# Two transformer blocks on one core: identity products ahead of the first weights, another order of the first loads, another list of order numbers

## The chip, the cores and the metric

The kernel runs on one core of a Trainium2 chip. Its engines work side by side, each through its own list of instructions in order: TensorE (PE in the profile, with its weight loads as PEld), VectorE (DVE), ScalarE (ACT), GpSimd (POOL) and SyncE (SP), which here only issues DMAs. The metric is the device time of one execution in microseconds (us). The kernel before takes 1480.22 us, the median of 3 runs (1479.65 to 1481.72).

## The reference

The input x is 32 sequences of 128 tokens with 256 features, in float32. Two transformer blocks follow one another. Both have 16 heads of 16, and both are conditioned by one vector for each sequence.

```
# block 1 (L0)
mod = silu(cond) @ ada_w + ada_b                 # shift, scale, gate, twice
x = x + gate_sa * (attention(ln(x) * (1 + scale_sa) + shift_sa) @ sa_proj_w + b)
x = x + cross_attention(ln(x), ctx, mask) @ ca_proj_w + b
x = x + gate_ff * (gelu((ln(x) * (1 + scale_ff) + shift_ff) @ fc1_w + b) @ fc2_w + b)
# block 2 (L1)
x = x + attention(adaln1(x, cond), rope on q and k) @ sa_out_w
x = x + cross_attention(adaln2(x, cond), ctx, rope) @ ca_out_w
x = x + (gelu(adaln3(x, cond) @ ffn_w1 + b) @ ffn_w2 + b)
```

## The kernel before

The batch is cut into 16 groups of two sequences, 256 tokens each. Eight streams are under way at a time. A stream carries one group through one block and then takes the next group, so that there are 32 passes (16 groups, two blocks). The second block's weights replace those of the first in the same tiles after the last use in the first block.

One pass has these steps. `normed_T` (line 527) makes the layer norm: statistics on VectorE, the power of -1/2 on GpSimd, the normalised `y` on VectorE (line 547), four transposes on TensorE (line 559), and the modulated copy `xt` (lines 577 and 579). `rows_T` (line 598) multiplies weights by `xt`, for q and k and for the first layer of the feed-forward; `values` (line 610) makes v. `attention` does the scores twice for each of the two sequences: once for the row maxima (lines 723 and 735), which a small transpose (line 748) turns and line 752 subtracts inside q, and once more for the exponentials (line 761). Line 769 multiplies the exponentials by the values. `over_sums` (line 780) divides by the sums: line 787 gathers the sums by DMA, line 792 takes the reciprocals, line 795 writes them to DRAM, line 800 reads them back with a broadcast in two DMAs, and line 803 multiplies. `project` (line 813) multiplies by the output weights (line 836). `fed_forward` is the last part.

**The order is made by a planner inside the kernel's own Python.** Each piece of work is a task, a generator that yields when it can start, on which engine, which slots it needs and its rank. `Clock` (line 41) keeps a planned time for each engine. It has a price for each instruction and each transfer, and `TURN` is added when TensorE goes from one kind of product to another (full; rows for the scores; columns for the exponentials by the values). `Tasks.run` (line 143) always takes the task that could start earliest on its engine. Among those that start about as early it takes the lowest rank. Instructions are issued in that order, so each engine's list is fixed when the kernel is built.

`ORDER` (line 35) disturbs this. The planned time is cut into stretches of `EVERY` = 40 us. Each stretch has a number in the list. At zero, the ranks are used as they are. Otherwise the number seeds a hash, which moves some tasks' ranks by -2 to +2, and its remainder by 4 picks the `patience`, the width of "about as early":

```python
at = int(min(t for e, t in clock.free.items() if e in ("pe", "dve", "act")) / EVERY)
seed = ORDER[at] if at < len(ORDER) else 0
patience = (0.02, 0.02, 0.3, 0.8)[seed % 4]
```

**The start.** SyncE issues the first loads at fixed places, ahead of all tasks: `rows` (line 284), the conditioning vector `embT_raw` (287), the column vectors `cols` (290), the first part of `ada_w` (313), the first group's x (317) and `qkv_w` (260, called from line 324). GpSimd makes the identity (line 328) and then fills the value tiles and the tiles for the maxima (lines 346 and 349); VectorE's first instruction is line 334, which needs `cols` and `rows`; ScalarE's is the silu of the conditioning vector (335), followed by copies of `rows` (353). `the_first` (line 461) multiplies `ada_w` by the silu in 16 products (line 448) for the first scale and shift. Then comes the first group's path through lines 547, 559, 579 and 598.

Of the kernel before, what the change touches and what calls it, by code (L numbers as in the profile page):

```python
# [10 lines left out]
F32 = mybir.dt.float32  # L11
U8 = mybir.dt.uint8
AF = mybir.ActivationFunctionType
ALU = mybir.AluOpType
# [3 lines left out]
P = 128  # L18
B, S, D, H, HD, DF = 32, 128, 256, 16, 16, 1024
KC = D // P  # L20
FC = DF // P
GB = 2
# [8 lines left out]
NEVER = 1e9  # L31
# [1 line left out]

EVERY = 40.0
ORDER = (
    200, 7, 0, 0, 0, 0, 297, 0, 0, 0, 0, 0, 0, 0, 0, 0, 129, 264, 0, 0, 0, 312, 0, 0, 0, 388, 0, 0, 109, 188, 182,
    0, 0, 0, 292, 58
)


class Clock:
# [1 line left out]


    HOP, DRAIN, TABLE, PACE = 0.06, 0.22, 1.28, 1.03
    TURN = {"full": 0.15, "rows": 0.1, "columns": 0.1}

    def __init__(self):
        self.free = dict.fromkeys(("pe", "dve", "act", "pool", "sp", "none"), 0.0)
# [7 lines left out]
    def use(self, engine, took, way="full"):  # L57

        if engine in ("exp", "gelu"):
            if engine != self.table:  # L60
                took += self.TABLE
                self.table = engine
            engine = "act"
        if engine == "pe":
            took = took * self.PACE + (self.TURN[way] if way != self.way else 0.0)
            self.way = way
        self.free[engine] = max(self.now, self.free[engine]) + took
        return self.free[engine] + (self.DRAIN if engine == "pe" else self.HOP)
# [154 lines left out]
def two_blocks(ctx: ExitStack, tc: tile.TileContext, a: dict, out: bass.AP):  # L223
    nc = tc.nc
# [4 lines left out]
    const = pool("const", 1)  # L229
# [3 lines left out]
    clock = Clock()  # L233
# [3 lines left out]
    mms = [psum.tile([P, 2 * GT], F32, name=f"products{i}") for i in range(3)]  # L237
# [24 lines left out]
    def weight(rows, cols, uses, *names):  # L262

        t = const.tile([P, rows // P, cols], F32, name=f"w_{names[0]}")

        def second():
            n = cols // len(names)
            for i, name in enumerate(names):
                load(t[:, :, i * n:(i + 1) * n], f"L1_xcond_{name}")
                end = clock.dma(6.0)  # L270
            return end

        return Weight(t, uses, second)
# [6 lines left out]
    w_fc1 = weight(D, DF, FC, "ffn_w1")  # L280
    w_fc2 = weight(DF, D, 1, "ffn_w2")

    rows = const.tile([P, C + 2], F32, name="rows")
    nc.sync.dma_start(out=rows, in_=a["rows"])

    embT = {name: const.tile([P, KC, B], F32, name=f"embT_{name}") for name in ("raw", "silu")}
    nc.sync.dma_start(out=embT["raw"], in_=a["cond_1024"])

    cols = const.tile([P, a["vectors"].shape[1]], F32, name="cols")
    nc.sync.dma_start(out=cols, in_=a["vectors"])  # L290
    for _ in range(3):
        clock.load(32)
    vectors, at = {}, 0
    for name in _VECTORS:
# [8 lines left out]
    c_fc1 = vectors["L0_xcond_fc1_b"]  # L303
    c_f1 = vectors["L1_xcond_ffn_b1"]


    ada_lo, late = w_fc1.t, w_fc2.t.rearrange("p (k n) d -> p k (n d)", k=KC)
    ada_hi = late[:, :, 0:2 * D]
    lnw = [late[:, :, 2 * D:], ada_lo[:, :, 0:2 * D], ada_hi]
    spare = [t.rearrange("p f n -> p (f n)") for t in ht]  # L310
    clock.slots["ht"] = [NEVER]
    src = a["L0_xcond_ada_w"].rearrange("(c p) n -> p c n", p=P)
    nc.sync.dma_start(out=ada_lo[:, :, 0:2 * D], in_=src[:, :, 0:2 * D])
    t_ada = clock.load(512)

    def load_x(t, src, g):
        nc.sync.dma_start(out=t, in_=src[g * GB:(g + 1) * GB].rearrange("b s d -> s b d"))

    def load_ctx(i, g):
        nc.sync.dma_start(out=cxs[i], in_=a["ctx_1024"].rearrange("(c p) n -> p c n", p=P)[:, :, g * GT:(g + 1) * GT])  # L320

    load_x(xs[0], a["x"], 0)
    t_x0 = clock.load(256)
    load(w_qkv.t, "L0_xcond_qkv_w")
    w_qkv.there[0] = clock.load(768)

    ident = const.tile([P, P], F32, name="ident")
    make_identity(nc, ident)
    neg_half = const.tile([P, GB], F32, name="neg_half")
    nc.gpsimd.memset(neg_half, -0.5)  # L330
    rope = const.tile([P, 2, 2, S], F32, name="rope")
# [127 lines left out]
    mods, gates, gates_at, biases = {}, {}, {}, {"fc2": r_fc2, "f2": r_f2}  # L459

    def the_first():
        t = max(t_ada, 6.5)
        scale = yield from modulation(t, 0, "sa_scale", ada_lo, "silu", c_ada, D, D, True)
        shift = yield from modulation(t, 0, "sa_shift", ada_lo, "silu", c_ada, 0, 0, False)
        mods["L0", "sa"] = scale, shift
# [198 lines left out]
    def plain(to, wm, w, src, t, bias):  # L664
        yield after(wm, w, t), "pe", "mm st", 3
        at = clock.take("st")
        st = sts[at]
        slot, ps, t = rows_T(w, 0, src, KC)
        there = Event()

        def move():
            yield t, "act", "", 1
            for c in range(KC):
                nc.scalar.activation(st[:, c, :], ps[:, c, :], AF.Identity, bias=bias[:, c:c + 1])
            end = clock.use("act", 0.84)
            clock.give("mm", slot, end)
            yield end, "sp", "", 1
            for e in range(2):
                nc.sync.dma_start(out=to[0:P:2, e:C:2, :], in_=st[64 * e:64 * e + 64, 0:KC, :])
                end = clock.dma(2.4)  # L680
            clock.give("st", at, there.add(end))

        tasks.spawn(move(), wm)
        return there

    def turned(to, wm, w, col, src, t):

        yield after(wm, w, t), "pe", "mm st", 3
        at = clock.take("st")
        st = sts[at].rearrange("p (a e) s -> p a e s", a=2)  # L690
        slot, ps, t = rows_T(w, col, src, KC)
        there = Event()

        def move():
            yield t, "dve", "", 1
            for b in range(GB):
                one = slice(b * S, (b + 1) * S)
                nc.vector.tensor_tensor(st[:, :, :, one], ps[:, :, one].unsqueeze(2).to_broadcast([P, 2, 2, S]), rope,  # L698
                                        ALU.mult)
            end = clock.use("dve", 1.25)  # L700
            clock.give("mm", slot, end)
            yield end, "pool", "", 1
            nc.gpsimd.tensor_tensor(st[:, 0], st[:, 0], st[:, 1], ALU.add)  # L703
            yield clock.use("pool", 1.27), "sp", "", 4
            for e in range(2):
                nc.sync.dma_start(out=to[2 * e:P:4, :, :], in_=st[:, 0, e, :])
                end = clock.dma(2.4)
            clock.give("st", at, there.add(end))

        tasks.spawn(move(), wm)  # L710
        return there

    def attention(wm, hd, masked, t, t_v, name, done):
# [66 lines left out]
        def over_sums():  # L780


            n, w = 4 * R, 4 * H * GT // P
            yield copied, "sp", "", 1
            o = ous[ou[0]]
            few = p_s.tile([P, w], F32, tag="few", name=f"few_{name}", bufs=3)
            nc.sync.dma_start(out=few, in_=o[1:P:8, :, :])
            at = clock.dma(2.2)
            nc.sync.dma_start(out=wm.xt, in_=o[0:P:2, :, :])
            clock.dma(2.0)  # L790
            yield at, "dve", "", 1
            nc.vector.reciprocal(few, few)
            yield clock.use("dve", 1.15), "sp", "", 1
            inv = dram2.tile([n, C * GT], F32, tag="inv", name=f"inv_{name}")
            nc.sync.dma_start(out=inv.rearrange("r (t w) -> (r t) w", w=w), in_=few)
            yield clock.dma(1.7), "sp", "", 1
            by = o[:, 0:KC, :]
            for c in range(2):
                half = inv[:, c * KC * GT:(c + 1) * KC * GT]
                nc.sync.dma_start(out=by[c:P:2, :, :], in_=half.unsqueeze(1).to_broadcast([n, 4, KC * GT]))  # L800
                at = clock.dma(2.2)
            yield at, "dve", "", 1.5
            nc.vector.tensor_tensor(wm.xt, wm.xt, by, ALU.mult)  # L803
            clock.give("ou", ou[0], done.add(clock.use("dve", 0.7)))
# [8 lines left out]
    def project(wm, x, lhs, n, w, ready, bias, gate, name):  # L813


        if bias is not None:
            bias = biases[bias]
        if gate is not None:
            y, gate = gate, ys[gate]
        if bias is not None:  # L820
            for b in range(GB):
                if gate is None:
                    nc.gpsimd.tensor_tensor(x[:, b, :], x[:, b, :], bias, ALU.add)
                else:
                    gb = p_s.tile([P, D], F32, tag="gb", name=f"gb_{name}_{b}", bufs=2)
                    nc.gpsimd.tensor_tensor(gb, gate[:, b, :], bias, ALU.mult)
                    nc.gpsimd.tensor_tensor(x[:, b, :], x[:, b, :], gb, ALU.add)
                    clock.use("pool", 0.7)
                clock.use("pool", 0.7)
# [64 lines left out]
    class Context:  # L894
# [5 lines left out]
        def fetch(self, wm):  # L900
            yield after(wm, w_kv, 0.0), "sp", "cx", 2
            self.slot = clock.take("cx")
            self.t = cxs[self.slot]
            load_ctx(self.slot, self.g)
            self.there.add(clock.dma(3.3))

    def attended(wm, at, x, masked, t, t_v, w, bias, gate, eps, mod, g, name, then, cx=None):

# [66 lines left out]
    def stream(wm, mine, loaded):  # L975

        while loaded:
# [12 lines left out]

            def next_x(i):
                load_x(xs[i], a["x"] if then < NG else middle, then % NG)
                return xs[i], clock.dma(3.3)

            if then is not None and clock.slot("x") < NEVER:
                other = clock.take("x")
# [111 lines left out]
```

## Time and profile before

| what | value |
|---|---|
| median of 3 runs | 1480.22 us |
| the profiled execution | 1490.8 us, its span 1488.7 us |
| granted TensorE clock, mean | 0.992 |
| weight loads of line 723, both kinds | 8192, 253.8 us |
| products of lines 598 and 836 with the feed-forward weights | 2048, 471.9 us |
| row maxima (line 735), VectorE | 256, 300.0 us |
| exponentials (line 761), ScalarE | 256, 248.2 us |

The profile is one execution; its span goes from the first to the last instruction. The 40 slices of the span show how evenly TensorE is used; a digit is the busy share in tenths.

```profile
PE   7998999999999999999999999999999999999998
DMA  6333223232223133133223241221223111212201
```

A row of the profile names the line of the kernel, the engine, the operation, and what is written and read (out<-in). Ends of products are modelled, since they are pipelined: consecutive products overlap in the rows.

### The profile page before, as it was taken

How to read it: one execution, taken by the hardware profiler on the slowest of the kernel's cores; microseconds unless marked ns; L12 is line 12 of the kernel's file. 1: busy time of each engine (PE TensorE's matmuls, PEld its weight loads, DVE VectorE, ACT ScalarE, POOL GpSimd, SP SyncE). 2: the span in 40 equal slices, each digit the busy share in tenths (PEclk: the TensorE clock that was granted, in tenths of full speed). 3: DMA queues.
4: the chain of work that ended last, by engine and by line, in shares of the span. 5: the costliest groups of instructions: out<-in, count | busy, mean ns of one | idle time of the engine just before them, and what ended most of it. 6: DMA issues, size and time to landing. Idle time of an engine off the chain costs nothing.

```text
span 1488.7 us, 39505 instructions
## 1 busy us (share of the span) xinstructions
PE 1441.7 (97%) x16992; PEld 1187.0 (80%) x16992; DVE 876.8 (59%) x1514; ACT 711.0 (48%) x1150; POOL 359.9 (24%) x498
## 2 busy tenths in 40 slices
PE   7998999999999999999999999999999999999998
PEld 6877778787888887887777887888788787887887
DVE  7664555545555545557468565566487557655531
ACT  6544545455555563544444534544444443544452
POOL 3031322421232322333123132122032121201110
PEclk9999999999999999999999999999999999999999
DMA  6333223232223133133223241221223111212201
GB/s 224 119 94 98 65 60 101 65 83 80 72 71 102 57 92 102 62 94 102 80 72 105 76 135 60 67 85 56 65 85 116 58 58 61 73 41 65 72 26 39
DMA packets 107358, 120.49 MB, mean 81 GB/s; under 512 B 11632, under 2 KB 82992, under 8 KB 107184
## 3 DMA queue, kind: packets, MB, share of 16 engines
q1 hardware_dynamic: 107184, 117.98, 25.7%
q8 instruction: 133, 2.18, 0.6%
q14 instruction: 41, 0.34, 0.1%
HBM read 54.92 MB, written 12.68 MB: 45 GB/s over the span
## 4 chain that ended last, share of the span: by engine, by line
PE 80%; DMA 7%; DVE 6%; SPq 2%; issue 2%; ACT 2%; POOL 1%; DVEq 0%; ACTq 0%; POOLq 0%
PE products L598 26%; PE products L836 22%; PE scores L723 15%; PE small L769 7%; PE products L610 6%; PE products L559 3%; DVE top L735 2%; DMA ou<-inv_a 1%; PE small L748 1%; ACT exp L761 1%; DVE xt L803 1%; DMA ou<-inv_d 1%; DMA ou<-inv_b 1%; PE products L448 1%; DVE y L547 1%
## 5 line engine op out<-in xcount | busy, mean ns | idle before, releaser
L761 ACT ACTIVATE exp<-scores 128x1024 f32<-128x1024 f32 x256 | 248.2, 1022 | 171.1 <-PE scores L723 161.3
L735 DVE TENSOR_REDUCE top<-scores 128x8 f32<-128x1024 f32 x256 | 300.0, 1214 | 45.1 <-PE scores L723 44.7
L598 PE MATMUL products<-xt,w_ffn_w 128*128 128x256 f32 x1024 | 238.5, 384 | 0.4 <-ACT ht L865 0.4
L836 PE MATMUL products<-w_ffn_w,ht 128*128 128x256 f32 x1024 | 233.4, 382 | 0.0
L836 PEld LDWEIGHTS products<-w_ffn_w,ht 128*128 128x128 f32 x1024 | 192.5, 191 | 28.5 <-issue 1.4
L598 PEld LDWEIGHTS products<-xt,w_ffn_w 128*128 128x128 f32 x1024 | 189.5, 190 | 31.9 <-issue 3.4
L723 PEld LDWEIGHTS scores<-qa,keys 32*128 32x128 f32 x4096 | 127.8, 188 | 52.4 <-issue 26.2
L865 ACT ACTIVATE ht<-products,cols 128x256 f32<-128x256 f32 x256 | 115.9, 473 | 105.6 <-PE products L598 104.6
L775 ACT COPY ou<-small 128x512 f32<-128x512 f32 x128 | 75.5, 590 | 189.3 <-PE small L769 187.6
L723 PE MATMUL scores<-qa,keys 32*128 32x128 f32 x4096 | 152.3, 285 | 10.1 <-DVE top L735 4.0
L723 PEld LDWEIGHTS scores<-keys,queries 32*128 32x128 f32 x4096 | 126.0, 186 | 37.7 <-issue 22.2
L723 PE MATMUL scores<-keys,queries 32*128 32x128 f32 x4096 | 150.5, 283 | 3.7 <-ACT exp L761 1.5
L769 PE MATMUL small<-exp,values 128*32 128x128 f32 x4096 | 138.4, 276 | 1.3 <-DVE qa L752 1.2
L703 POOL TENSOR_TENSOR st<-st 128x512 f32<-128x512 f32 x64 | 83.4, 1307 | 232.0 <-DVE st L698 211.2
L841 DVE TENSOR_TENSOR x<-products,x 128x512 f32<-128x512 f32 x64 | 44.1, 689 | 142.5 <-PE products L836 141.8
L598 PE MATMUL products<-xt,w_qkv_w 128*128 128x256 f32 x512 | 125.7, 392 | 0.8 <-DVE xt L579 0.8
L752 DVE TENSOR_TENSOR qa<-queries,small 128x512 f32<-128x512 f32 x128 | 86.9, 679 | 63.9 <-PE small L748 61.2
L769 PEld LDWEIGHTS small<-exp,values 128*32 128x32 f32 x4096 | 104.0, 109 | 24.0 <-issue 11.4
L598 PEld LDWEIGHTS products<-xt,w_qkv_w 128*128 128x128 f32 x512 | 96.7, 196 | 16.4 <-issue 2.0
L803 DVE TENSOR_TENSOR xt<-xt,ou 128x512 f32<-128x512 f32 x64 | 48.8, 762 | 93.9 <-DMA ou<-inv_a 32.5
L698 DVE TENSOR_TENSOR st<-products,rope 128x512 f32<-128x512 f32 x128 | 81.5, 684 | 13.7 <-PE products L598 9.7
L845 DVE TENSOR_TENSOR y<-products,y 128x512 f32<-128x512 f32 x32 | 22.1, 689 | 108.4 <-PE products L836 92.8
(109 smaller groups left out, 1761.6 us busy)
## 6 DMA issues: line engine op xcount, KB each, us to landing
xt<-ou SPq DMA_DIRECT2D x64, 256.0 KB
keys<-st SPq DMA_DIRECT2D x96, 128.0 KB
queries<-st SPq DMA_DIRECT2D x96, 128.0 KB
cxt<-in_ctx SPq DMA_DIRECT2D x32, 256.0 KB
x<-in_x SPq DMA_DIRECT2D x16, 256.0 KB
keys<-st SPq DMA_DIRECT2D x16, 256.0 KB
y<-gate_dram_sa SPq DMA_DIRECT2D x16, 256.0 KB
ou<-inv_a SPq DMA_DIRECT2D x32, 128.0 KB
```

The costliest lines, as they stand in the source:

```text
L598: nc.tensor.matmul(ps[:, c, :], lhsT=w.t[:, k, at:at + P], rhs=src[:, k, :], start=(k == 0), stop=(k == KC - 1))
L610: nc.tensor.matmul(ps[:, b, :], lhsT=src[:, k, b * S:(b + 1) * S], rhs=w.t[:, k, col:col + D], start=(k == 0), stop=(k == KC - 1))
L698: nc.vector.tensor_tensor(st[:, :, :, one], ps[:, :, one].unsqueeze(2).to_broadcast([P, 2, 2, S]), rope, ALU.mult)
L703: nc.gpsimd.tensor_tensor(st[:, 0], st[:, 0], st[:, 1], ALU.add)
L723: nc.tensor.matmul(sc[:, r, c * S:(c + 1) * S], lhsT=lhs(slice(32 * r, 32 * r + 32), c), rhs=rhs(slice(32 * r, 32 * r + 32), c), start=Tru ...
L735: nc.vector.tensor_reduce(top[:, r:r + 2, TOP:TOP + 2 * C:2], scs[slot][:, r:r + 2, :].rearrange("p r (c s) -> p r c s", s=S), AX.X, ALU.max)
L752: nc.vector.tensor_tensor(qa, q[:, :, cut], ps.unsqueeze(1).to_broadcast([P, C, S]), ALU.subtract)
L761: nc.scalar.activation(exps[pt][r // 2], scs[slot][:, r:r + 2, :], AF.Exp, scale=SCALE)
L769: nc.tensor.matmul(ats[at][32 * r:32 * r + 32, c * S:(c + 1) * S], lhsT=v[:, b, i:i + HD, :].rearrange("p d t -> p (d t)"), rhs=exps[pt][r ...
L775: nc.scalar.copy(ous[ou[0]][:, :, cut], ats[at].rearrange("p (c s) -> p c s", s=S))
L836: nc.tensor.matmul(ps[:, b, :], lhsT=lhs(k, b), rhs=w.t[:, k, :], start=(k == 0), stop=(k == n - 1))
L865: nc.scalar.activation(ht[f // (FC // 2)][:, f % (FC // 2), :], ps[:, 0, :], AF.Gelu, bias=b1[:, f:f + 1])
```

## The change

The change has four parts.

- Twelve products of the identity by itself are put on TensorE right after the identity is made. They write a products buffer that nothing reads before it is written again.
- The first loads go out in another order: `embT_raw`, `ada_w`, `rows`, the first x, `cols`, `qkv_w`.
- Prices of the planner are set anew: `TURN`, now by the kind that is left rather than entered; several transfers; and the earliest start of `the_first`, 5.5 for 6.5.
- `ORDER` is a new list, of 37 numbers, 26 of them not zero, where the old one has 36 with 12 not zero.

In `project` a task may also wait, in the planner only, for a bias row that has not been planned yet.

```diff
-    200, 7, 0, 0, 0, 0, 297, 0, 0, 0, 0, 0, 0, 0, 0, 0, 129, 264, 0, 0, 0, 312, 0, 0, 0, 388, 0, 0, 109, 188, 182,
-    0, 0, 0, 292, 58
+    6622, 0, 91896, 0, 27754, 24892, 69964, 0, 30721, 66120, 0, 41605, 0, 69433, 0, 43084, 27437, 27178, 72830,
+    16201, 38328, 98324, 37276, 0, 13032, 79752, 41486, 59529, 18013, 48897, 61204, 13263, 51033, 0, 0, 0, 0
...
-    TURN = {"full": 0.15, "rows": 0.1, "columns": 0.1}
+    TURN = {"full": 0.1, "rows": 0.15, "columns": 0.15}
...
-            took = took * self.PACE + (self.TURN[way] if way != self.way else 0.0)
+            took = took * self.PACE + (self.TURN[self.way] if way != self.way else 0.0)
...
-                end = clock.dma(6.0)
+                end = clock.dma(3.0)
...
+    nc.sync.dma_start(out=embT["raw"], in_=a["cond_1024"])
+    clock.load(32)
...
+    nc.sync.dma_start(out=ada_lo[:, :, 0:2 * D], in_=src[:, :, 0:2 * D])
+    t_ada = clock.load(512)
     rows = const.tile([P, C + 2], F32, name="rows")
     nc.sync.dma_start(out=rows, in_=a["rows"])
...
+    load_x(xs[0], a["x"], 0)
+    t_x0 = clock.load(256)
     nc.sync.dma_start(out=cols, in_=a["vectors"])
-    for _ in range(3):
+    for _ in range(2):
         clock.load(32)
...
     make_identity(nc, ident)
+
+    for _ in range(12):
+        nc.tensor.matmul(mms[0][:, 0:P], lhsT=ident, rhs=ident, start=True, stop=True)
...
-        t = max(t_ada, 6.5)
+        t = max(t_ada, 5.5)
...
             nc.sync.dma_start(out=few, in_=o[1:P:8, :, :])
-            at = clock.dma(2.2)
+            at = clock.dma(2.1)
             nc.sync.dma_start(out=wm.xt, in_=o[0:P:2, :, :])
-            clock.dma(2.0)
+            clock.dma(2.4)
...
-            yield clock.dma(1.7), "sp", "", 1
+            yield clock.dma(1.6), "sp", "", 1
...
-                at = clock.dma(2.2)
+                at = clock.dma(2.5)
...
-            bias = biases[bias]
+            if bias not in biases:
+                yield (lambda: 0.0 if bias in biases else NEVER), "none", "", 0
+            row = biases[bias]
```

Left out are the old places of the moved lines, the renaming of `bias` to `row` in its uses, and four more prices of transfers: 2.4 to 2.3 twice, for the moves of keys and queries (lines 680 and 707); 3.3 to 3.0 for the context; and 3.3 to 2.9 for the next x.

More of the change, by code (lines that the diff above doesn't have):

```diff
@@ L281, in two_blocks, with load_x @@
     w_fc2 = weight(DF, D, 1, "ffn_w2")
+    embT = {name: const.tile([P, KC, B], F32, name=f"embT_{name}") for name in ("raw", "silu")}
+    nc.sync.dma_start(out=embT["raw"], in_=a["cond_1024"])
+    clock.load(32)
+    ada_lo, late = w_fc1.t, w_fc2.t.rearrange("p (k n) d -> p k (n d)", k=KC)
+    ada_hi = late[:, :, 0:2 * D]
+    lnw = [late[:, :, 2 * D:], ada_lo[:, :, 0:2 * D], ada_hi]
+    src = a["L0_xcond_ada_w"].rearrange("(c p) n -> p c n", p=P)
+    nc.sync.dma_start(out=ada_lo[:, :, 0:2 * D], in_=src[:, :, 0:2 * D])
+    t_ada = clock.load(512)
     rows = const.tile([P, C + 2], F32, name="rows")
     nc.sync.dma_start(out=rows, in_=a["rows"])
-    embT = {name: const.tile([P, KC, B], F32, name=f"embT_{name}") for name in ("raw", "silu")}
-    nc.sync.dma_start(out=embT["raw"], in_=a["cond_1024"])
     cols = const.tile([P, a["vectors"].shape[1]], F32, name="cols")
+    def load_x(t, src, g):
+        nc.sync.dma_start(out=t, in_=src[g * GB:(g + 1) * GB].rearrange("b s d -> s b d"))
+    load_x(xs[0], a["x"], 0)
+    t_x0 = clock.load(256)
     nc.sync.dma_start(out=cols, in_=a["vectors"])
-    for _ in range(3):
+    for _ in range(2):
         clock.load(32)
@@ L304, in two_blocks @@
     c_f1 = vectors["L1_xcond_ffn_b1"]
-    ada_lo, late = w_fc1.t, w_fc2.t.rearrange("p (k n) d -> p k (n d)", k=KC)
-    ada_hi = late[:, :, 0:2 * D]
-    lnw = [late[:, :, 2 * D:], ada_lo[:, :, 0:2 * D], ada_hi]
     spare = [t.rearrange("p f n -> p (f n)") for t in ht]
     clock.slots["ht"] = [NEVER]
[L312 to L317, printed above, removed]
     def load_ctx(i, g):
         nc.sync.dma_start(out=cxs[i], in_=a["ctx_1024"].rearrange("(c p) n -> p c n", p=P)[:, :, g * GT:(g + 1) * GT])
-    load_x(xs[0], a["x"], 0)
-    t_x0 = clock.load(256)
     load(w_qkv.t, "L0_xcond_qkv_w")
@@ L679, in move @@
                 nc.sync.dma_start(out=to[0:P:2, e:C:2, :], in_=st[64 * e:64 * e + 64, 0:KC, :])
-                end = clock.dma(2.4)
+                end = clock.dma(2.3)
             clock.give("st", at, there.add(end))
@@ L706, in move @@
                 nc.sync.dma_start(out=to[2 * e:P:4, :, :], in_=st[:, 0, e, :])
-                end = clock.dma(2.4)
+                end = clock.dma(2.3)
             clock.give("st", at, there.add(end))
@@ L822, in project @@
                 if gate is None:
-                    nc.gpsimd.tensor_tensor(x[:, b, :], x[:, b, :], bias, ALU.add)
+                    nc.gpsimd.tensor_tensor(x[:, b, :], x[:, b, :], row, ALU.add)
                 else:
                     gb = p_s.tile([P, D], F32, tag="gb", name=f"gb_{name}_{b}", bufs=2)
-                    nc.gpsimd.tensor_tensor(gb, gate[:, b, :], bias, ALU.mult)
+                    nc.gpsimd.tensor_tensor(gb, gate[:, b, :], row, ALU.mult)
                     nc.gpsimd.tensor_tensor(x[:, b, :], x[:, b, :], gb, ALU.add)
@@ L904, in fetch @@
             load_ctx(self.slot, self.g)
-            self.there.add(clock.dma(3.3))
+            self.there.add(clock.dma(3.0))
     def attended(wm, at, x, masked, t, t_v, w, bias, gate, eps, mod, g, name, then, cx=None):
@@ L992, in next_x @@
                 load_x(xs[i], a["x"] if then < NG else middle, then % NG)
-                return xs[i], clock.dma(3.3)
+                return xs[i], clock.dma(2.9)
             if then is not None and clock.slot("x") < NEVER:
```

## The prediction

> **What bounds the kernel now.** I read the page first: busy shares and the chain of waits by engine.
>
> ```profile
> span 1488.7 us, 39505 instructions
> PE 1441.7 (97%) x16992; PEld 1187.0 (80%) x16992; DVE 876.8 (59%) x1514; ACT 711.0 (48%) x1150; POOL 359.9 (24%) x498
> PE 80%; DMA 7%; DVE 6%; SPq 2%; issue 2%; ACT 2%; POOL 1%; DVEq 0%; ACTq 0%; POOLq 0%
> ```
>
> TensorE (PE) is the bound. The change leaves every product of the reference in place, so it can gain only from PE's idle time and its slow clock. PE is idle for 1488.7 - 1441.7 = 47.0 us: 8.0 in the first 40 us, 4.7 in the last 9, and about 34.5 between. Next, PE's own waits in the summary of waits:
>
> ```profile
> PE products L836 <- DVE xt L803: 10.5, 12, 2.9
> PE products L559 <- DVE y L547: 6.0, 6, 2.4
> PE scores L723 <- ACT exp L761: 5.0, 7, 1.4
> PE scores L723 <- DVE top L735: 4.6, 6, 2.6
> ```
>
> (Columns: us in total, times, longest.) PE runs its instructions in the order written. These waits are the places where the planner put a product ahead of its operand. The largest is the end of `over_sums`, whose last step is the broadcast of line 800. Third, the granted clock, in stretches cut at the edges of its falls (us, PE busy and count, clock, DMA):
>
> ```profile
> 6.99:10.40 3.41, 2.79 (x14) 1.00 1.05 374
> 13.82:17.23 3.41, 3.41 (x10) 1.00 0.78 267
> 194.72:198.13 3.41, 2.00 (x49) 1.00 0.63 159
> 727.20:730.62 3.42, 1.79 (x45) 1.00 0.38 121
> 730.62:734.03 3.41, 3.41 (x9) 0.50 0.23 81
> ```
>
> A stretch of 3.41 us with PE busy for 1.79 is followed by one at half clock; one with 2.00 is not. There are six such falls between 40 us and the end, one of them of two stretches: 7 x 3.41 = 23.9 us at half clock, of which 1.1 idle, so (23.9 - 1.1) / 2 = 11.4 us lost. The orderable loss is thus 34.5 + 11.4 = 46 us, 3% of the span. (Before 17.23 us the clock has no record and prints 1.00. The pace says half: 16 products x 256 columns take 5.96 us from 12.65, later eight take 1.89.)
>
> **The start.** The timeline of the first 13 us (start, duration):
>
> ```profile
> 2.11 0.43 SPq L313 DMA_DIRECT2D w_ffn_w<-in_L_xcond_ada_w  x1
> 3.75 2.91 DVE L334 TENSOR_SCALAR c_q_even<-cols,rows 128x4 f32<-128x4 f32 x1 [3.75 <-DMA cols<-in_vectors]
> 6.19 3.59 PE L448 MATMUL products<-embT_silu,w_ffn_w 128*128 128x32 f32 x16 [6.19 <-DMA w_ffn_w<-in_L_xcond_ada_w]
> 6.44 0.19 POOL L349 MEMSET top<- 128x128 f32 x1
> 6.75 0.43 DVE L534 BATCH_NORM_STATS2 st_a<-x 128x6 f32<-128x256 f32 x1
> 9.82 0.41 DVE L455 TENSOR_SCALAR mod_sa_shift<-products,cols 128x32 f32<-128x32 f32 x2 [1.30 <-PE products L448]
> 10.15 0.73 DVE L547 TENSOR_SCALAR y<-x,mv_a,rstd_a 128x256 f32<-128x256 f32 x2
> ```
>
> *Loads.* The weights of the modulation were the fourth load (issued at 2.11) and become the second: 1.18. The chain gives 3.95 us from issue to landing, so 5.13 instead of 6.06, and the 16 products run 5.26 to 8.85. `mod_sa_shift` comes at about 8.9 instead of 9.82 and stops being last: `rstd_a` on POOL ends at 9.01 (8.30 + 0.71), and it hangs on the statistics at 6.75. `y` then starts at about 9.25 instead of 10.15: **0.9 us earlier**, and the transposes with it. Can the statistics start earlier too? The first x is issued 0.5 us sooner. But L334 stands ahead on VectorE. It took 2.91 us for four columns and ended at 6.66, just after POOL's run of memsets (6.44 + 0.19 = 6.63), which does not move. I keep 6.75. The load `cols` drops from third to fifth place. It lands behind the first x, at about 6.3, still before 6.63, so the memsets hide it. If 2.91 us is instead L334's own length, it ends at 9.2 and `y` is 1.5 us later than now. So the start lies between -1.9 (statistics early) and +1.5, and I take -0.9. `rows` lands 1.3 us later; ScalarE's copies (L353) follow it, covered by ScalarE's idle 3.60 us before line 643. SyncE issues the same six loads in the same time.
>
> *Twelve products of the identity.* The identity is ready at 1.29 us. Nearest rows: 16 products with 128-column weight loads in 3.59 us (0.22 each) and four transposes in 1.23 (0.31 each), so 2.7 to 3.7 us, done by 4.0 to 5.0, before 5.13: no cost. Their use would be a full clock from the first product on. Upper bound: transposes 0.6, and the slow part of L598 (12.65 to 17.23, half of 4.58 = 2.3), 2.9 us in all. The Trainium skill ("TensorE: Matmul & The Clock Gate", "What's actually happening") wants about 3.4 us of sustained activity for the full clock and, once there, tolerates idling up to about 3 us ("Why this matters for your kernels"). By the rule, 2.7 us of products fall short, but products and modulation might do it together, and the lull after them (8.85 to 9.7, then 1.2 of transposes, 0.8 idle) would keep it: -2.9. The rows are stricter on both sides. The stretch 6.99 to 10.40, busy for 2.79 with these same modulation products, did not raise the clock, a full one from 13.82 did. And 1.79 busy of 3.41 already lost it, with one lull of 1.63 us. I go by the rows: the clock stays low or falls again before L598, **0**.
>
> **The order.** `ORDER` holds one number for each 40 us of the planner's time; zero leaves the ranks alone. I take the trace's 40 us stretches for the planner's. Past the first, 11 stretches have a number now and 24 have none. The stretch table, summed over each kind:
>
> ```profile
> sum 440.00, PE 432.44; mean PE 39.31
> sum 960.00, PE 933.68; mean PE 38.90
> ```
>
> Idle is 0.69 us in a stretch with a number and 1.10 in one without. Half-clock time is 0.50 and 0.77 us, half of it lost, so 0.25 and 0.38. Together a numbered stretch loses 0.54 us less. The new list has 25 numbers past the first: 14 more, 14 x 0.54 = **7.6 us**. This is a rate carried over from 11 stretches, not a mechanism; without it the order is worth 0, and a bad draw costs (below).
>
> The planner's prices of transfers change as well; they are not instructions. The one that counts is line 800, 2.2 to 2.5. In the chain of waits the second of its two transfers takes, when it is on the chain:
>
> ```profile
> 127.45 2.52 DMA ou<-inv_a
> 151.16 2.90 DMA ou<-inv_a
> 581.59 5.11 DMA ou<-inv_a
> ```
>
> So 0.3 more covers only the shortest. At most it takes 0.3 us from each of the 12 waits on L803: 3.6 us. These waits are inside the 46 us, so I do not add it. `TURN` moves cost from entering to leaving a kind of product; a full-rows-full excursion is 0.25 before and after: 0. The `biases` wait is the planner's and issues nothing: 0.
>
> **Sum.** 0.9 + 7.6 = 8.5 us against the profiled execution: 1490.8 (its span and 2.1 around it) becomes 1482.3. The plain runs' median is 1480.22, so scale by 1480.22 / 1490.8 = 0.993: **1471.8, say 1472 us**.
>
> **Rivals.**
> - *The falls of the clock halve* (0.20). The six waits that made them, 2.86, 2.41, 1.55, 1.63, 2.59 and 1.71, sum to 12.7; half-clock costs 7 x 1.7 = 11.9. Half of that is 12.3; with 0.9 and at most 3.6 from line 800 it is 16.8: 1480.2 - 16.7 = 1464. For it: one avoided wait of 1.6 us saves 3.3. Against: no price of the planner knows the clock.
> - *The numbers are luck of the draw* (0.12): four of the eleven numbered stretches still lose over 0.8 us. Then only the start counts: 1479, no change to speak of.
> - *More work is put behind `over_sums` than it can bear* (0.18). Place: L836 behind L803. The chain shows transfers of line 800 of 3.9 us against 2.5 in the plan: a wait of 1.4 and a fall at 1.7, 3.1 us each. Two falls more than the present six cost 6.2, less 0.9: 1480.2 + 5.3 = 1485.5. It decides from the first extra fall on (3.1 against 0.9). For it: with 25 fresh numbers nearly every meeting of transfers on SyncE's queue is new. Against: the price of line 800 rises, which puts L836 later.
> - The forecast itself 0.50.
>
> Loss per stretch (its idle time and half of its half-clock time, the 35 rows of the stretch table) scatters by about 1.8 us, over 35 stretches about 10.6, so 8 times in 10 within 13.6 of the forecast: 1458 to 1486, which holds both outer cases. A measurement tells 0.2% (3 us) from no change. Faster 0.70, same 0.12, slower 0.18.
>
> **What would show it.** Start: first modulation product near 5.2 us, first L598 near 11.7, at half pace (eight in about 3.4 us). If they run eight in 1.9, I am wrong on the clock. If `c_q_even` ends well after 6.7, wrong on VectorE. Order: PE idle between 40 us and the last stretch falls from 34.5 to about 29, falls from six to four or five. Over 40 idle or eight falls is the slow rival.

## The result and the profile after

The changed kernel takes 1469.54 us, the median of 5 runs (1467.35 to 1470.9), against 1481.72 us for the kernel before (5 runs): a ratio of 0.992, 95% interval [0.9902, 0.9939], or 12.2 us less. The prediction was 1472 us.

The page of the changed kernel, the lines that answer to those shown of before (span, busy engines, chain of waits by engine):

```profile
span 1465.5 us, 39524 instructions
PE 1433.2 (98%) x17016; PEld 1183.2 (81%) x17016; DVE 883.9 (60%) x1546; ACT 700.6 (48%) x1120; POOL 356.3 (24%) x498
PE 75%; DMA 8%; DVE 8%; issue 3%; POOL 2%; SPq 2%; ACT 2%; DVEq 0%; ACTq 0%; POOLq 0%
```

TensorE is still the bound. Its idle time went from 47.0 to 32.3 us (1465.5 - 1433.2). It has 24 instructions more, for 12 identity products; they count as busy. PE's own waits after (us in total, times, longest):

```profile
PE products L565 <- DVE y L553: 8.0, 7, 3.3
PE products L844 <- DVE xt L809: 5.9, 8, 1.3
...
PE scores L729 <- ACT exp L767: 0.4, 2, 0.2
```

Lines moved by 6 to 8: L565 is the old 559, L844 the old 836, L809 the old 803. The waits behind `over_sums` fell from 10.5 to 5.9 us, those of the scores behind the exponentials from 5.0 to 0.4. The wait for `y` rose from 6.0 to 8.0 us; one wait of 2.1 us is at the start.

The clock, in stretches cut at its edges (us, PE busy and count, clock, DMA):

```profile
1.36:4.77 3.41, 3.41 (x16) 1.00 0.72 219
4.78:8.19 3.41, 2.84 (x26) 1.00 0.97 330
8.19:11.60 3.41, 1.08 (x5) 1.00 1.03 322
11.60:15.02 3.42, 3.42 (x9) 0.50 1.07 376
366.59:370.00 3.41, 1.59 (x33) 1.00 0.41 117
479.23:482.64 3.41, 1.61 (x9) 1.00 0.30 103
```

The first row has no clock record and prints 1.00; the count tells the pace: 16 instructions in 3.41 us, then 26 in 2.84. The identity products did raise the clock, at 4.78 us. After the lull it fell again, at 11.60. Beyond the start the clock falls twice, after the two last rows; in the profile before it fell six times. These are single executions; what all runs show of the clock stands with the table of the orders below.

### The profile page after: what moved, and what is told of

Same layout as the page of the kernel before. It is cut to its first block, busy times and chain, and to the rows that moved or that the text cites. A ratio compares the mean times of both kernels' runs of the same rounds, so it can differ in the third digit from the quotient of the medians.

```text
span 1465.5 us, 39524 instructions
## 1 busy us (share of the span) xinstructions
PE 1433.2 (98%) x17016; PEld 1183.2 (81%) x17016; DVE 883.9 (60%) x1546; ACT 700.6 (48%) x1120; POOL 356.3 (24%) x498
## 4 chain that ended last, share of the span: by engine, by line
PE 75%; DMA 8%; DVE 8%; issue 3%; POOL 2%; SPq 2%; ACT 2%; DVEq 0%; ACTq 0%; POOLq 0%
PE products L604 24%; PE products L844 20%; PE scores L729 15%; PE small L775 7%; PE products L616 5%; PE products L565 3%; DVE top L741 2%; DMA ou<-inv_d 1%; PE small L754 1%; DMA inv_d<-few_d 1%; DMA few_d<-ou 1%; DVE st L704 1%; ACT exp L767 1%; SPq L806 1%; DMA ou<-inv_a 1%
## 5 line engine op out<-in xcount | busy, mean ns | idle before, releaser
L844 PE MATMUL products<-w_ffn_w,ht 128*128 128x256 f32 x1024 | 231.9, 381 | 0.0
L844 PEld LDWEIGHTS products<-w_ffn_w,ht 128*128 128x128 f32 x1024 | 191.8, 190 | 27.5 <-issue 0.8
L775 PEld LDWEIGHTS small<-exp,values 128*32 128x32 f32 x4096 | 104.3, 109 | 24.2 <-issue 11.6
L624 ACT COPY values<-products 128x512 f32<-128x512 f32 x64 | 40.0, 626 | 122.1 <-PE products L616 120.0
L809 DVE TENSOR_TENSOR xt<-xt,ou 128x512 f32<-128x512 f32 x64 | 48.2, 754 | 81.5 <-DMA ou<-inv_b 26.2
L704 DVE TENSOR_TENSOR st<-products,rope 128x512 f32<-128x512 f32 x128 | 81.8, 680 | 21.8 <-PE products L604 14.8
```

Source lines behind the costliest of these rows:

```text
L775: nc.tensor.matmul(ats[at][32 * r:32 * r + 32, c * S:(c + 1) * S], lhsT=v[:, b, i:i + HD, :].rearrange("p d t -> p (d t)"), rhs=exps[pt][r ...
L844: nc.tensor.matmul(ps[:, b, :], lhsT=lhs(k, b), rhs=w.t[:, k, :], start=(k == 0), stop=(k == n - 1))
```

## Experiments: the start or the order

Two kernels split the change. **The order alone** keeps the changed kernel's issues and takes back the loads and the products; the planner's calls stay, so that the order stays. Its edit:

```diff
-    for _ in range(12):
-        nc.tensor.matmul(mms[0][:, 0:P], lhsT=ident, rhs=ident, start=True, stop=True)
...
+    # loads issued as before: rows, embT, cols, ada_w, x, qkv_w
```

> The changed kernel with its order of issues untouched, but the first loads in the old order and without the identity products. The theory that the order of the issues carries the gain expects 1470 to 1472 us (10 to 11 of the 12.2 us stay), with PE idle after 40 us near 23 us. The rival, that the new start carries it through the clock and the earlier first product, expects 1477 to 1481 us.

Measured: 1472.59 us, ratio 0.9925 [0.99, 0.995]. **The start alone** puts the new loads and the products into the kernel before:

```diff
-    nc.sync.dma_start(out=rows, in_=a["rows"])
     nc.sync.dma_start(out=embT["raw"], in_=a["cond_1024"])
+    nc.sync.dma_start(out=w_fc1.t[:, :, 0:2 * D], in_=src[:, :, 0:2 * D])
+    nc.sync.dma_start(out=rows, in_=a["rows"])
+    nc.sync.dma_start(out=xs[0], in_=a["x"][0:GB].rearrange("b s d -> s b d"))
...
+    for _ in range(12):
+        nc.tensor.matmul(mms[0][:, 0:P], lhsT=ident, rhs=ident, start=True, stop=True)
```

> The kernel before with its own order of issues, but the new order of the first loads and the twelve identity products. The theory that the order carries the gain expects 1479 to 1481 us (1 to 2 us faster than before) with the first L598-type product near 11.4 us. The rival expects 1470 to 1474 us. If the earlier start is swallowed by the first waits after it, 1481 to 1482.

Measured: 1481.93 us, ratio 0.9998 [0.9982, 1.0014]: between 2.7 us faster and 2.1 slower. By the ratios (times 1481) the order carries 11.1 of 11.9 us; the start can't be told from nothing. Its timeline shows that the start did come earlier:

```profile
1.35 4.74 PE L332 MATMUL products<-ident 128*128 128x128 f32 x24 [1.35 <-POOL ident masks.py:199]
...
11.15 5.80 PE L602 MATMUL products<-xt,w_qkv_w 128*128 128x256 f32 x16 [0.82 <-DVE xt L583]
16.87 1.05 PE L476 MATMUL products<-w_ffn_w,embT_silu 128*32 128x256 f32 x4
```

The last row began at 18.54 in the kernel before, 1.67 us later. Whether the whole run keeps that lead is below what the times resolve.

**Without the products**, loads new:

> The changed kernel without the identity products; loads in the new order. My prediction's step (the products are worth nothing at the end) expects 1469 to 1471 us: the modulation starts at about 5.1 and ends at 8.6 us at half pace, the first normalised y still waits for the statistics and starts near 9.2, and the first 256-column products start near 11.4. The rival, that the products buy a full clock, expects 1472 to 1473 us.

Measured: 1473.25 us, ratio 0.9939 [0.9915, 0.9962], by the ratios 2.8 us slower than the whole change, give or take 4.4: not resolved. In its timeline the modulation runs at half pace, and `mod_sa_shift` is last again before `y`:

```profile
5.61 3.60 PE L451 MATMUL products<-embT_silu,w_ffn_w 128*128 128x32 f32 x16 [5.61 <-DMA w_ffn_w<-in_L_xcond_ada_w]
9.24 0.41 DVE L458 TENSOR_SCALAR mod_sa_shift<-products,cols 128x32 f32<-128x32 f32 x2 [1.14 <-PE products L451]
```

The first qkv product then starts at 12.08 us; with the products it is 11.38. At that point of the profiles the products bring 0.7 us and not zero.

**A bridged start** fills the lull, too:

```diff
         mods["L0", "sa"] = scale, shift
+        for _ in range(8):
+            nc.tensor.matmul(ats[0][:, 0:P], lhsT=ident, rhs=ident, start=True, stop=True)
...
                 nc.tensor.transpose(ps[:, c, b, :], xn[:, b, c * P:(c + 1) * P], ident)
+        if mod == ("L0", "sa") and g == 0:
+            for _ in range(3):
+                nc.tensor.matmul(ats[0][:, 0:P], lhsT=ident, rhs=ident, start=True, stop=True)
```

> The changed kernel with eleven more identity products: eight between the modulation and the first transposes, three after those transposes, so that PE has no lull before the first 256-column products. If a lull is what lets the clock fall again at 11.6 us, the sixteen products from 11.4 us take 3.5 us instead of 5.4, and the time is 1.5 to 2 us lower: 1467.5 to 1468. If the products cost PE time or the gain is lost at the next wait, 1469.5 or more.

Measured: 1470.97 us, ratio 0.9917 [0.9895, 0.9939], no different from the change. Its timeline:

```profile
7.73 2.03 PE L473 MATMUL small<-ident 128*128 128x128 f32 x16
11.39 3.93 PE L609 MATMUL products<-xt,w_qkv_w 128*128 128x256 f32 x16 [0.15 <-DVE xt L590]
15.25 1.05 PE L480 MATMUL products<-w_ffn_w,embT_silu 128*32 128x256 f32 x4
20.92 1.17 PE L734 MATMUL scores<-keys,queries 32*128 32x128 f32 x32 [0.98 <-DMA keys<-st]
```

The clock stays up: the sixteen products take 3.93 us instead of 5.41, and the next row starts at 15.25 instead of 16.72. Of this lead of 1.47 us, 0.98 is lost at 20.92, where the first scores wait for the DMA of the keys.

## Experiments: the numbers or the planner

My forecast took a number in `ORDER` to be worth 0.54 us wherever it stands. These kernels change only the list, or the list and the prices. "Planner's end" is the time of the last product in the planner's own account of the kernel. It is no measurement; the question is how far the chip follows it.

**The new list in the kernel before**, nothing else changed:

> The kernel before, whole, with the new list of numbers in place of its own: 26 numbers under the old prices and the old start. My prediction's step (a stretch with a number loses 0.54 us less than one without, whatever the number) expects 1472 to 1476 us. The rival, that a list is worth something only in the planner in which it was searched, and that the chip follows the planner's end, expects that end (1503.3, where the old list gives 1457.3 and 1481.7 on the chip) to carry over: 1525 to 1530 us.

**No numbers** (`ORDER = ()`) in the kernel before:

> The kernel before with an empty list, so that no rank is disturbed. My prediction's step (eleven numbers past the first at 0.54 us) expects 1487 to 1489 us. If the chip follows the planner's end (1484.1 against 1457.3), 1506 to 1511 us. If the numbers are luck on the chip, 1475 to 1490 us.

**A list searched for the old prices**, in the changed kernel with the old prices (the earliest start of `the_first` stays at 5.5):

> The changed kernel with all prices of the planner as before, and a list searched anew for those prices (planner's end 1453.1, against 1457.3 of the old list; replayed under the new prices this order ends at 1458.2, the old order at 1461.5, the new at 1450.1). If the chip follows the planner's end under either set of prices, the gain is 3 to 5 us: 1477 to 1479. If the new prices are what makes an order hold on the chip, none of it arrives: 1481 to 1485. If any newly searched list does as well as the new one, 1468 to 1472.

**A list from a shorter search**, new prices:

> The changed kernel, new prices, with another list from a shorter search (planner's end 1462.8; the old order replayed under these prices ends at 1461.5, the new at 1450.1). If the chip follows the planner's end, 1480 to 1484 us, no faster than before. If the new prices alone give the gain, 1468 to 1473.

**Two numbers** (71933 in the first stretch, 23413 in the eleventh, the first two of the list searched for the old prices), old prices:

> The changed kernel with the old prices and a list with two numbers only, in the first and the eleventh stretch (planner's end 1458.2, the old list's 1457.3). My prediction's rate (0.54 us a number past the first) would put it 5 us behind the old list and ahead of nothing: 1485 to 1488. If the chip follows the planner's end to the microsecond, it is level with the old order: 1480 to 1484. If orders with about the same planned end scatter on the chip by several us, and the old list is one that came out badly, 1469 to 1476.

What they gave. Idle is PE's from 40 us to the end of the profile, and half clock is the time at half pace before the last product of that profile. The column behind it is a mean over all runs: the span and the mean granted clock of each run are on record, and 2 x (1 - clock) x span is its time at half clock (24 us for the profile of the kernel before).

| order | numbers | planner's end, own prices | idle, us | half clock, us | half clock, mean of all runs | ratio to before, interval |
|---|---|---|---|---|---|---|
| before | 12 | 1457.3 | 39.0 | 23.9 | 10.2 (69 runs) | 1 |
| before, start alone | 12 | 1457.3 | 39.3 | 17.1 | 15.0 (14) | 0.9998 [0.9982, 1.0014] |
| changed kernel | 26 | 1450.1 | 27.6 | 10.2 | 12.3 (5) | 0.992 [0.9902, 0.9939] |
| new list in the kernel before | 26 | 1503.3 | 71.7 | 51.2 | 55.4 (2) | 1.0416 [1.0392, 1.044] |
| no numbers | 0 | 1484.1 | 67.5 | 41.0 | 38.0 (2) | 1.0285 [1.0262, 1.0309] |
| searched for the old prices | 9 | 1453.1 | 28.8 | 6.8 | 11.7 (6) | 0.9926 [0.9909, 0.9943] |
| shorter search, new prices | 12 | 1462.8 | 30.5 | 10.2 | 17.0 (14) | 0.9953 [0.994, 0.9965] |
| two numbers, old prices | 2 | 1458.2 | 33.5 | 17.1 | 14.7 (6) | 0.9954 [0.9937, 0.997] |

The idle column comes from the stretch from 40 us to the end (its length, then PE busy). First the kernel before, then the changed one, then that with two numbers, then that without any:

```profile
40.00:1488.70 1448.70, 1409.71 (x16783) 0.99 0.25 77
```

```profile
40.00:1465.50 1425.50, 1397.92 (x16704) 1.00 0.25 79
```

```profile
40.00:1474.50 1434.50, 1401.00 (x16759) 1.00 0.25 78
```

```profile
40.00:1522.50 1482.50, 1415.01 (x16794) 0.99 0.24 75
```

Four things follow. The same 26 numbers cost 62 us in the planner they were not searched for (1541.65 us): a number has no worth of its own. Two numbers gain 6.8 us over the list of twelve: their count says nothing. The new prices are not needed: a list searched for the old ones gains 11 us. And the chip follows the planner's end over tens of us, but not over the last few. The old list and the two numbers are planned 1 us apart, in the other direction, and lie 6.8 us apart on the chip. The shorter search came out at 1472.78 us, 7.0 us faster than the old list. From its planned end I had expected 1480 to 1484; 1468 to 1473, my other case, was for the new prices alone giving the gain, and the list for the old prices shows that they aren't needed.

What the time does follow is the idle column. From the old order (39.0 and 39.3) it falls by 5.6 for the two numbers, 8.7 for the shorter search, 10.4 for the old prices and 11.6 for the changed kernel. The times fall by 6.8, 7.0, 11.0 and 11.9 us (ratio times 1481). Without the falls of the clock, idle time explains the tuned orders within 2 us; the two untuned ones lose 28 and 33 us of idle and 42 and 62 us of time. Half of their extra time at half clock (38.0 and 55.4 against 10.2) is 14 and 23 us, an estimate of what it costs, since the modulation took 3.60 us at half pace and 1.87 at full. Idle and clock together then make 42 and 55 us.

The falls of the clock are a small part of the gain. The profile before, with 24 us at half clock, was not typical: the mean of 69 runs is 10.2. With the same start, the new order has 4.3 us less (the order alone has 5.9 in 6 runs) or, with the new start, 2.7 less (15.0 to 12.3): by the same estimate 1 to 2 us of the 11. The rows with the new start can't be set against the first row in this column, for that profile has no record of the slow clock of its first 17 us.

## Experiments: are the falls of the clock a cost of their own

Identity products were put in front of the longest waits, where PE would sit idle, so that the clock stays up. PE tasks are counted in the planner's loop; a products buffer that the planner has free takes them:

```diff
+            if task[1][1] == "pe":
+                if self.products in FILL:
+                    self.fill(FILL[self.products])
+                self.products += 1
             self.waiting.remove(task)
...
+    def fill(n):
+        at = clock.slots["mm"]
+        i = at.index(min(at))
+        if at[i] <= clock.now:
+            for _ in range(n):
+                nc.tensor.matmul(mms[i][:, 0:P], lhsT=ident, rhs=ident, start=True, stop=True)
```

In the kernel before:

> The kernel before, its order and loads untouched, with identity products put on PE in front of the fourteen places where its profile shows PE waiting longest after 100 us: 2 to 10 products each, sized to fit into the wait. PE's waits stay, but PE is not idle in them. If the falls of the clock are a cost of their own (two profiles of this order show 26.6 and 19.5 us at half clock, 2.5 of it after the last product), they go from the middle and the time falls by 6 to 11 us: 1470 to 1475, which is most of what the change brought. If the falls cost nothing beyond the waits, or the products only lengthen the waits, 1480 to 1484.

In the changed kernel and in that with the old prices, both with the bridged start as well:

> The changed kernel with the bridged start and identity products in front of nine waits that its profiles show (3 to 14 products each). Half clock in its profiles is 6.5 to 12.1 us, 1.5 to 3 of it at the end. If the falls are a cost of their own, 1465 to 1468 us; if not, 1469.5 to 1472.

> The list searched for the old prices, with the bridged start and identity products in front of thirteen waits that its profile shows. That profile has 8.1 us at half clock, so there is less to win: if the falls are a cost of their own 1464 to 1467 us, if not 1468 to 1471.

Measured: 1486.42 us, ratio 1.0034 [1.0022, 1.0045]; 1469.8 us, 0.9915 [0.9903, 0.9927]; 1469.41 us, 0.9918 [0.9905, 0.9931]. None is shown to be faster than the kernel that it fills, and the first is 5 us slower. The clock did rise in all three: half clock, as the mean of all runs, went from 10.2 to 4.8 us (15 runs), from 12.3 to 4.7 (5) and from 11.7 to 3.5 (5). By the estimate above that is worth 3 to 4 us, and something else took it back, with 5 us more in the first kernel. So covering the waits brought no time; that a fall costs nothing is not shown. Among the runs of one kernel those with the lower clock are longer, by 0.42 us for each us at half clock (161 runs, all kernels), though a run that waits longer may also fall more often.

The profile of the first kernel has 3.4 us at half clock before the last product. Two of its stretches, which the kernel before had with 35.90 and 39.45 us busy:

```profile
120.00:160.00 40.00, 39.85 (x519) 1.00 0.36 105
340.00:380.00 40.00, 37.45 (x495) 1.00 0.30 88
```

In the first, where the kernel before had a clock of 0.91, it is 1.00. In the second PE idles 2.0 us more, with no such products there. The timeline names one place:

```profile
349.75 1.10 PE L842 MATMUL products<-w_sa_out_w,xt 128*128 128x256 f32 x4 [1.36 <-DVE xt L809]
```

In the kernel before the same product waited 0.18 us (at 353.48). PE came earlier and its operand did not. That part of the lead is given back. It does not explain why the runs of this kernel are slower than before: its profiled execution (1482.52 us, span 1480.4) is the fastest of its 15 runs, so it shows less than their loss. Products that overrun a wait that is shorter in another run would do it, and so would products that wait themselves: in this profile two of them waited 1.8 us in all for a copy (L624) that still read their buffer. No profile here settles it, and it stays open. No kernel of the study is shown to beat the changed one.

## Why the prediction was right in size, and where its working was not

**Bound and direction: right.** PE idle after 40 us was what changed, by 11.4 us in the profiles (39.0 to 27.6). Between 40 us and the last stretch I had put its fall at 34.5 to about 29; it went to 23.2.

**The order, 7.6 us: the size came out near by luck (11.1 measured with loads and products taken back, 7.4 to 14.8 by the interval), the reason was wrong.** The failed step is the one that read off "a numbered stretch loses 0.54 us less" and multiplied it by 14. The stretch table of the changed kernel, first the 25 stretches with a number, then the 10 without, turns the rate round:

```profile
sum 1000.00, PE 979.54; mean PE 39.18
sum 400.00, PE 397.26; mean PE 39.73
```

Idle is 0.82 us in a stretch with a number and 0.27 in one without. The numbers of a list act together: each changes what all later ones meet. What the runs showed instead is a whole order with less idle time on PE.

**The half-clock term was over-read.** I counted six falls and 11.4 us from one profile. That execution took 1490.8 us, 10 over the median, and had more than twice the half clock of the mean run: 10.2 us, of which half, about 5, is lost. The same order with the new start shows three falls after 40 us. The stretches do not lie alike in each execution: with the two numbers a fall at 10.91 us puts their edges at 4.09 and 7.50, not at 1.36 and 4.77, and the same 24 identity instructions took 5.49 us, not 4.57.

**The start, 0.9 us: near in the trace, not resolved in the times.** `y` was forecast for about 9.25 and began at 9.22, the qkv products for 11.7 and began at 11.38. The statistics did hold it, though 0.2 us later than forecast, at 6.93: L340, which waits for `cols`, could start at 6.73, not 6.3. Line 334 (now L340) took 0.29 us there, after the memsets:

```profile
6.73 0.29 DVE L340 TENSOR_SCALAR c_q_even<-cols,rows 128x4 f32<-128x4 f32 x1 [6.73 <-DMA cols<-in_vectors]
6.93 0.42 DVE L540 BATCH_NORM_STATS2 st_a<-x 128x6 f32<-128x256 f32 x1
9.22 0.73 DVE L553 TENSOR_SCALAR y<-x,mv_a,rstd_a 128x256 f32<-128x256 f32 x2 [0.52 <-POOL rstd_a L547]
```

So its 2.91 us before were the wait for GpSimd's memsets, and the bad end of +1.5 us is out. Other traces agree: where it starts before the memsets are done, from 3.53 to 6.45 us, it takes from 3.13 down to 0.29 us and ends at 6.65 to 6.74 in each, and the last memset at 6.62 to 6.66.

**The identity products: cost and use both mis-sized.** I priced twelve at 0.22 us and had them end by 5.0. One product in float32 is two instructions: the twelve are 24, and the modulation's 16 are eight products. They kept PE from 1.34 to 5.75, when the modulation began. Without them it began at 5.61, as soon as its weights were there, so against that trace they cost 0.14 us; the weights landed at 5.47 there (1.18 + 4.29) and not at 5.13. In return a full stretch raised the clock at 4.78, and the modulation took 1.87 us instead of 3.60. "Low or falls again before the qkv products" was nearly right in its second half: it fell at 11.60, 0.22 us after they began, with about eight of the sixteen at half pace. For the time of the whole run, value zero is neither shown nor refuted: the kernel without the products is 2.8 us slower, give or take 4.4.

**Rivals.** The slow one, two falls more, did not come: there are two in place of six. "The falls halve" came in part, with 4.3 and 2.7 us less at half clock in the means, and carries 1 to 2 us. "The numbers are luck" was meant as no gain; in another sense it is near the truth, since orders planned 1 us apart came out 6.8 us apart. What makes the old list one that holds badly on the chip is open.

## What to carry to other kernels

A searched list of seeds has no worth by the entry: it belongs to the planner, prices and start that it was searched with, and a change of any of them means a new search. Judge an order by TensorE's idle time in the trace, read the clock as a mean over several runs and not from one profile, and expect plans a few us apart to scatter by as much on the chip; so keep several candidates and run them. An engine made faster at the start wins only as far as the next wait that another engine or a DMA sets: 0.98 of 1.47 us were gone within 6 us.

## What the runs showed of the hardware

The clock fell after stretches of 3.41 us with PE busy for 1.59, 1.61 and 1.79 us and held after one with 2.00. Single waits of 1.63 us (before, from 727.20) and 1.82 us (after, from 366.59) were enough. But busy time alone sets no limit, as a stretch of the list for the old prices and one of the two numbers show:

```profile
260.50:263.91 3.41, 1.42 (x7) 1.00 0.53 162
55.28:58.69 3.41, 2.09 (x41) 1.00 0.38 142
```

After the first, with a wait of 2.27 us, the clock stayed at 1.00; after the second it fell to 0.50. What else counts, no run here shows. "TensorE: Matmul & The Clock Gate" of the Trainium skill ("Why this matters for your kernels") allows gaps of about 3 us; the two waits above were shorter, and where they differ the traces decide. Its warm-up agrees ("What's actually happening", about 3.4 us): after one full stretch of identity products, 1.36 to 4.77 us, the modulation took 1.87 us, and without them 3.60.
